# Bias seeded into the accumulation banks by ACT, in place of additions on GpSimd, in a two-layer graph kernel

## The chip, the cores and the metric

The kernel runs on one core of a Trainium2 chip. The metric is the device time of one execution in microseconds. Engines are named as in the profile: PE is TensorE's matmul, PEld its weight load, DVE is VectorE, ACT is ScalarE, POOL is GpSimd, SP is SyncE, which here only issues DMAs.

## The reference

There are 64 graphs of 256 nodes with 512 features, and one 256 x 256 adjacency matrix of zeros and ones. Two layers follow each other, each with a residual:

```python
h = jnp.maximum(_layernorm(x, axis=-1), 0.0)
# layer 0: masked scores, divided by the norm of their row
q, k, v = (jnp.einsum('bnd,ed->bne', h, W) for W in (Wq, Wk, Wv))
rel = adjacency.T[None, :, :] * jnp.einsum('bnd,bmd->bnm', q, k)
rel = rel / jnp.linalg.norm(rel, axis=2, keepdims=True)
x = x + jnp.einsum('bnm,bmd->bnd', rel, v)
h = jnp.maximum(_layernorm(x, axis=-1), 0.0)
# layer 1
y = jnp.einsum('nm,bmd->bnd', adj, h)
x = x + jnp.einsum('bnd,do->bno', y, weight) + bias
```

The last line holds what the change is about: the product of y with the weight, the bias of 512 values, and the addition to x.

## The kernel before

Work goes by pairs of graphs: 32 pairs, each of 512 rows in four chunks of 128 (TC = 4). Operands of products are split into three parts called u, l and s (upper, lower, and a third one for the cross terms), and `three` makes each product out of three passes over four chunks of the inner dimension, 12 matmuls of 512 columns, into one PSUM bank of 128 x 512.

`unit` is the frame of such a block. It takes the next of eight banks in rotation (`next_bank`), puts in the passes u and l, then an activation on ACT that multiplies the bank by ONE in place (L331), then the pass s, then a drain. The pass s of one block is recorded only after the passes u and l of the next block, so the scaling lies under other matmuls.

A pair goes through these stages:

- `h_rows`: statistics of the rows of the next pair on DVE (L259, L260, L263), then on ACT the square root (L265) and the normalised rows (L273).
- `g_stage`: four blocks of G, from h and a product of the query and key weights; each is split by ACT (gy_u, L232) and DVE (gy_s, L233, and gy_l, L235).
- `v_stage`: four blocks of V, two before and two after the scores, split in the same way into v_low and late_parts.
- `scores`: two blocks from G and h with 256 columns a matmul (h_u,gy_u, then h_l,gy_l, then hs,gy_s), multiplied on DVE by the adjacency (L406), their squares summed on ACT (L410) in the same bank.
- `turn_scores`: the scores turned by 16 DMAs on SP (L446) and DVE transposes (L452), and split (L462 to L464). In the first two pairs and the last one PE turns them.
- `attend`: four blocks of scores times V; DVE scales each by the row's norm and adds it to x in the tile `x_ring` (L487). There are two such tiles in turn.
- `layer_1`: statistics of the new x, then the normalised rows into `rel_s_raw` (L273), split by ACT (L507) and DVE (L508). After that POOL adds the bias, broadcast to 128 partitions in `bias_bc`, to each chunk of x (L511).
- `gather`, one pair late: four blocks that multiply by the adjacency, split by ACT (L241) and DVE (L242, L243) into the gy tiles again.
- `mix`, one pair late: four blocks of gy times the weight (w_u,gy_u; w_l,gy_l; w_s,gy_s); DVE adds each bank to x (L549). `store` writes x out by a DMA that POOL issues (L558).

The order of the instructions is not written by hand. Every step is recorded in a `Plan` with its engine, a cost in us, and keys that it reads and writes. `order` gives PE's steps due times by their own order and costs, works back to due times for all that they need, and then lists each engine's steps as they come ready, earliest due first. The engines run these lists in order, so a step that waits holds up all that stand behind it on its engine.

At the start the bias comes by a DMA on ACT's queue (L575) and is left alone until L511. Two versions of the pairs are compiled, for adjacencies that can and cannot be held exactly in the short format; this run takes the first, in which the tiles are called adjt_r and late_parts.

Of the kernel before, what the change touches and what calls it, by code (L numbers as in the profile page):

```python
# [12 lines left out]
AF = mybir.ActivationFunctionType  # L13
# [100 lines left out]
def kernel(  # L114
# [93 lines left out]
    V, A, G, SP = nc.vector, nc.scalar, nc.gpsimd, nc.sync  # L208
    count = {"bank": 0}

    def next_bank():
        n = count["bank"] % 8
        count["bank"] += 1
        return bank[n], ("bank", n)

    placed_all = [("blocks", j, k) for j in range(P // S) for k in range(P // S)]
# [102 lines left out]
        while waiting:  # L319
            waiting.pop(0)()  # L320

    def unit(plan, first, second, drain):

        ps, key = next_bank()
        for cost, fn, reads in first(ps):
            plan.add("PE", cost, fn, reads, [key])
        finish(plan)
        if second is None:
            drain(ps, key)
            return  # L330
        plan.add("ACT", 0.49, lambda: A.activation(ps, ps, AF.Copy, scale=ONE), [], [key])  # L331

        def rest():
            for cost, fn, reads in second(ps):
                plan.add("PE", cost, fn, reads, [key])
            drain(ps, key)
        waiting.append(rest)

    def three(left, right, names_l, names_r, cost, outs=None):


        def group(k, ds, begin):
            def first(ps):
                for d in ds:
                    for n, (o, lf, rt) in enumerate(outs(ps, k, d) if outs else [(ps, left(k, d), right(k, d))]):
                        mm(o, lf, rt, begin and d == ds[0] and n == 0)
            return first

        def first(ps):
            for k, ds, begin in ((0, (0, 1), True), (0, (2, 3), False), (1, (0, 1, 2, 3), False)):  # L350
                yield cost * len(ds), (lambda go=group(k, ds, begin): go(ps)), [
                    n for d in ds for n in (*names_l(k, d), *names_r(k, d))]

        def second(ps):
            ds = (0, 1, 2, 3)
            yield cost * len(ds), (lambda go=group(2, ds, False): go(ps)), [
                n for d in ds for n in (*names_l(2, d), *names_r(2, d))]
        return first, second
# [56 lines left out]
    def turn_scores(plan, i, by_pe=False):  # L415
        rn, name = norms[i % 2], f"rn{i % 2}"
        sums = [(name, b, k) for b in range(NB) for k in range(NC)]
        plan.add("ACT", 0.2, lambda: A.activation(rn, rn, AF.Sqrt), [], sums)
        plan.add("DVE", 0.12, lambda: V.reciprocal(rn, rn), [], sums)
        if by_pe:  # L420
            u, l = (part.rearrange("p b t k n -> p b (t k n)") for part in rel_p)
            for b in range(NB):
                ps, key = next_bank()

                def go(ps=ps, b=b):
                    for t in range(NC):
                        for k in range(NC):
                            nc.tensor.transpose(ps[:, ts(t * NC + k, P)], rel[:, b, k, ts(t, P)], ident)

                def third(b=b):  # L430
                    V.scalar_tensor_tensor(rel_third()[:, b].rearrange("p t k n -> p (t k n)"),
                                           f(l[:, b]), CROSS, f(u[:, b]), op0=ALU.mult, op1=ALU.subtract)
                plan.add("PE", 0.44, go, [("h_rel", b)], [key])
                plan.add("ACT", 0.49, lambda ps=ps, b=b: A.activation(
                    u[:, b], ps, AF.Copy, scale=NEAR), [key], [("rel_u", b)])
                plan.add("DVE", 0.63, lambda ps=ps, b=b: V.tensor_sub(
                    l[:, b], ps, f(u[:, b])), [key, ("rel_u", b)], [("rel_l", b)])
                plan.add("DVE", 0.6, third, [("rel_u", b), ("rel_l", b)],
                         [("raw", 0), ("raw", 1)] if not b else [("raw", 1)])
            return  # L440
        rv = rel.rearrange("p b k (t m) -> p (b k t) m", m=P)
        pv = placed.rearrange("p b k t n -> p (b k t) n")

        for j in range(P // S):
            for k in range(P // S):
                plan.add("SP", 0.65, lambda j=j, k=k: SP.dma_start(  # L446
                    out=pv[ts(j, S), :, ts(k, S)], in_=rv[ts(k, S), :, ts(j, S)]),
                    [("h_rel", 0), ("h_rel", 1)], [("placed", j, k)], lands=2.1)
        halves, rel_u, rel_l = ([(name, b) for b in range(NB)] for name in ("raw", "rel_u", "rel_l"))
        for b in range(NB):  # L450
            for k in range(NC):
                plan.add("DVE", 0.33, lambda b=b, k=k: V.transpose(  # L452
                    raw()[:, b].rearrange("p (t k n) -> p t k n", t=NC, k=NC)[:, :, k], placed[:, b, k]),
                    [("placed", j, t) for j in range(P // S) for t in range(P // S)] + [("h_rel", 2), ("h_rel", 3)], halves if not b and not k else halves[b : b + 1])

        def whole(ap):
            return ap.rearrange("p b t k n -> p (b t k n)")

        def flat_raw():
            return raw().rearrange("p b d -> p (b d)")  # L460
        u, l = (whole(part) for part in rel_p)
        plan.add("ACT", 0.96, lambda: A.activation(u, flat_raw(), AF.Copy, scale=NEAR), halves, rel_u)  # L462
        plan.add("DVE", 1.14, lambda: V.tensor_sub(l, flat_raw(), f(u)), [*halves, *rel_u], rel_l)
        plan.add("DVE", 1.14, lambda: V.scalar_tensor_tensor(  # L464
            whole(rel_third()), f(l), CROSS, f(u), op0=ALU.mult, op1=ALU.subtract), [*rel_u, *rel_l], halves)
# [28 lines left out]
    def layer_1(plan, i, exact):  # L494
        slot = i % 2
        relu, needs = norm(plan, i, 1, ring[slot], f"x{slot}")
        for c in range(TC):
            x_c = [(f"x{slot}", c), *needs]
            if not exact:
                plan.add("ACT", 0.72, lambda c=c: relu(changing("late", "h2", 8, D)[:, c], c), x_c,  # L500
                         keys("late", 12)[4:] if not c else [("late", 4 + c)])
                continue
            u, l = 3 + 2 * c, 4 + 2 * c
            k = [("raw", c % 2)]
            plan.add("ACT", 0.72, lambda c=c: relu(raw()[:, c % 2], c), x_c,
                     [("raw", 0), ("raw", 1)] if not c else k)
            plan.add("ACT", 0.53, lambda c=c, u=u: A.copy(late(u), raw()[:, c % 2]), k, [("late", u)])  # L507
            plan.add("DVE", 0.6, lambda c=c, u=u, l=l: V.tensor_sub(  # L508
                late(l), raw()[:, c % 2], f(late(u))), [*k, ("late", u)], [("late", l)])
        for c in range(TC):  # L510
            plan.add("POOL", 1.4, lambda c=c: G.tensor_tensor(  # L511
                ring[slot][:, c, :], ring[slot][:, c, :], bias_bc, ALU.add), [], [(f"x{slot}", c)])

    def gather(plan, i, exact):
        right = adjt[0]
# [24 lines left out]
    def mix(plan, i, blocks_of=range(4)):  # L540
        slot = i % 2
        for c in blocks_of:
            b = c // NC
            first, second = three(
                lambda k, d, c=c: gy[k][:, d, ts(c, P)], lambda k, d: w_p[k][:, d, :],
                gy_half(b), named("w_u", "w_l", "w_s"), MM)

            def drain(ps, key, c=c):
                plan.add("DVE", 0.6, lambda: V.tensor_add(  # L549
                    ring[slot][:, c, :], ps, ring[slot][:, c, :]), [key], [(f"x{slot}", c)])  # L550
                if i + 1 == NP:
                    plan.add("SP", 0.65, lambda: SP.dma_start(
                        out=outs[i][:, c, :], in_=ring[slot][:, c, :]), [(f"x{slot}", c)], [], lands=3.0)
            unit(plan, first, second, drain)

    def store(plan, i):
        slot = i % 2
# [60 lines left out]
    def first_turn(plan):  # L618

        u, l = h  # L620
        for d in range(DC):
            ps, key = next_bank()

            def go(ps=ps, d=d):
                for c in range(TC):
# [30 lines left out]

    def turn_wv(plan):
        for d in range(DC):
            ps, key = next_bank()

            def go(ps=ps, d=d):
                for e in range(DC):
                    nc.tensor.transpose(ps[:, ts(e, P)], wv_sb[:, e, ts(d, P)], ident)
            plan.add("PE", 0.44, go, placed_all, [key])
            split_right_ps(plan, ps, key, [lambda at, q=q: q[:, at, :] for q in wv_p],
                           [[("wv_u", d)], [("wv_l", d)], [("wv_s", d)]], d)
# [6 lines left out]
    def pairs(exact):  # L673
# [20 lines left out]
        h_turn(plan)  # L694
        h_parts(plan)
        split_w(plan)
        attend(plan, 0, exact)
        for i in range(1, NP):
            last = i + 1 == NP
# [63 lines left out]
```

## Time and profile before

| what | value |
|---|---|
| median of 3 runs | 1596.04 us (1594.61 to 1597.64) |
| the profiled execution | 1595.87 us |
| its span, first to last instruction | 1594.1 us |
| granted TensorE clock | 0.999 |
| instructions on PE, DVE, ACT, POOL | 8046, 2419, 1812, 167 |
| busy time of POOL, L511 alone | 216.2 us, 191.4 us |
| ACT's in-place scaling, L331 | 572 times, 581 ns each |
| reads and writes of HBM | 65 GB/s over the span |

Busy time of an engine is the union of its instructions. The end of a matmul is modelled, so PE can be called busy where the next matmul starts late; times lost on PE are read from the starts of matmuls in the timeline. A matmul of 512 columns appears as 128x512, its weights as 128x128. An entry like `x_ring<-bank,rn,x_ring` names what is written and what is read. Behind the bar stands the time that an engine sat idle before the group, and whom it waited for.

### The profile page before, as it was taken

The page shows a single profiled execution, that of the slowest core. Times are in us where ns is not written, and L with a number is a line of the kernel's source. Part 1 is how long each engine was busy: PE and PEld are TensorE (multiplying, and loading weights), DVE is VectorE, ACT ScalarE, POOL GpSimd, SP SyncE. Part 2 cuts the span into 40 slices and gives each one's busy share as a digit, 9 for nine tenths or more (in the row PEclk, how much of TensorE's full clock was granted, in tenths as well). Part 3 has the DMA queues.
Part 4 walks back from the last instruction along what each step waited for, and adds up shares of the span by engine and source line. Part 5 has one row for each costly group of instructions (what it writes and reads, how often), then busy time and mean ns, then how long its engine had stood idle before and what let it go on. Part 6 is the DMA issues. An engine that isn't in the chain of part 4 may idle for free.

```text
span 1594.1 us, 22542 instructions
## 1 busy us (share of the span) xinstructions
PE 1566.8 (98%) x8046; PEld 1327.2 (83%) x8046; DVE 1423.1 (89%) x2419; ACT 953.1 (60%) x1812; POOL 216.2 (14%) x167
## 2 busy tenths in 40 slices
PE   9999999999999999999999999999999999999998
PEld 6788888888888888888888888888888888888886
DVE  6998899988998988998989999889989889989886
ACT  5566566565566565665665565656665656656553
POOL 0011111011111011110111110111100111101111
PEclk9999999999999999999999999999999999999999
DMA  6421444324444334443234442344432344433311
GB/s 193 111 77 44 115 110 119 65 74 113 112 114 99 77 79 117 109 117 71 75 108 114 112 119 62 76 115 110 116 94 72 87 118 109 118 65 80 81 54 56
DMA packets 433130, 153.64 MB, mean 96 GB/s; under 512 B 389872, under 2 KB 390128, under 8 KB 433008
## 3 DMA queue, kind: packets, MB, share of 16 engines
q1 hardware_dynamic: 422784, 116.46, 30.9%
q0 software_dynamic: 8432, 32.51, 5.5%
q10 hardware_dynamic: 1792, 3.15, 0.5%
q8 instruction: 65, 1.06, 0.3%
q14 instruction: 57, 0.47, 0.1%
HBM read 70.78 MB, written 33.55 MB: 65 GB/s over the span
## 4 chain that ended last, share of the span: by engine, by line
DVE 43%; PE 42%; ACT 5%; SPq 4%; DMA 3%; issue 2%; DVEq 0%; ACTq 0%
PE bank L222 42%; DVE st L259 7%; DVE gy_l L235 7%; DVE x_ring L487 5%; DVE late_parts L508 5%; DVE gy_s L233 5%; DVE hs L302 4%; SPq L446 3%; DVE x_ring L549 2%; DVE mv L260 2%; ACT rel_s_raw L273 2%; SPq L287 1%; ACT gy_u L232 1%; DVE h_l L312 1%; DMA fresh<-in_x_dram 1%
## 5 line engine op out<-in xcount | busy, mean ns | idle before, releaser
L331 ACT ACTIVATE bank<-bank 128x512 f32<-128x512 f32 x572 | 332.3, 581 | 395.7 <-PE bank L222 393.3
L511 POOL TENSOR_TENSOR x_ring<-x_ring,bias_bc 128x512 f32<-128x512 f32 x128 | 191.4, 1515 | 382.3 <-ACT rel_s_raw L273 382.3
L558 POOL DMA_DIRECT2D out_dram<-x_ring x31 | 24.0, 774 | 978.5 <-DVE x_ring L549 978.5
L222 PE MATMUL bank<-wv_s,hs 128*128 128x512 f32 x512 | 138.5, 392 | 0.4 <-ACT bank L331 0.4
L222 PE MATMUL bank<-w_u,gy_u 128*128 128x512 f32 x512 | 138.0, 391 | 0.0
L222 PE MATMUL bank<-wv_u,h_u 128*128 128x512 f32 x512 | 137.7, 391 | 0.0
L222 PE MATMUL bank<-w_s,gy_s 128*128 128x512 f32 x512 | 137.4, 390 | 0.4 <-ACT bank L331 0.4
L222 PE MATMUL bank<-w_l,gy_l 128*128 128x512 f32 x512 | 137.4, 390 | 0.0
L222 PE MATMUL bank<-wv_l,h_l 128*128 128x512 f32 x512 | 137.3, 390 | 0.0
L222 PE MATMUL bank<-h_u,m_u 128*128 128x512 f32 x512 | 136.5, 389 | 0.3 <-DVE m_s L233 0.3
L222 PE MATMUL bank<-h_l,m_l 128*128 128x512 f32 x512 | 136.6, 389 | 0.1
L222 PE MATMUL bank<-hs,m_s 128*128 128x512 f32 x512 | 136.3, 389 | 0.0
L233 DVE SCALAR_TENSOR_TENSOR gy_s<-gy_u,bank 128x512 fp32r<-128x512 f32 x128 | 86.0, 674 | 41.9 <-ACT gy_u L232 41.8
L235 DVE SCALAR_TENSOR_TENSOR gy_l<-gy_s,gy_u 128x512 fp32r<-128x512 f32 x128 | 113.7, 890 | 4.3
L273 ACT ACTIVATE rel_s_raw<-x_ring,nb,rs 128x512 f32<-128x512 f32 x128 | 100.6, 810 | 24.9 <-DVE late_parts L508 15.6
L222 PE MATMUL bank<-adjt_r,late_parts 128*128 128x256 f32 x896 | 115.1, 280 | 0.0
L222 PEld LDWEIGHTS bank<-w_s,gy_s 128*128 128x128 f32 x512 | 95.9, 188 | 21.1 <-ACT bank L331 1.1
L222 PEld LDWEIGHTS bank<-w_u,gy_u 128*128 128x128 f32 x512 | 96.0, 188 | 20.8
L222 PEld LDWEIGHTS bank<-w_l,gy_l 128*128 128x128 f32 x512 | 96.1, 188 | 20.7
L222 PEld LDWEIGHTS bank<-wv_l,h_l 128*128 128x128 f32 x512 | 96.1, 188 | 20.5
L222 PEld LDWEIGHTS bank<-h_u,m_u 128*128 128x128 f32 x512 | 96.0, 188 | 20.5 <-ACT wv_u L232 0.5
L222 PEld LDWEIGHTS bank<-h_l,m_l 128*128 128x128 f32 x512 | 96.0, 188 | 20.4 <-DVE h_l L312 0.5
(109 smaller groups left out, 3226.9 us busy)
## 6 DMA issues: line engine op xcount, KB each, us to landing
fresh<-in_x_dram SPq DMA_DIRECT2D x31, 1024.0 KB, 5.9
blocks<-h_rel SPq DMA_DIRECT2D x496, 64.0 KB, 2.1
x_ring<-in_x_dram SPq DMA_DIRECT2D x31, 1024.0 KB, 7.9
out_dram<-x_ring POOLq DMA_DIRECT2D x31, 1024.0 KB, 5.4
h_rel<-h_rel SPq DMA_DIRECT2D x464, 32.0 KB, 1.9
blocks<-in_L_gnn_Wv_dram ACTq DMA_DIRECT2D x1, 1024.0 KB, 10.9
x_ring<-in_L_gnn_weight_dram SPq DMA_DIRECT2D x1, 1024.0 KB, 12.5
out_dram<-x_ring SPq DMA_DIRECT2D x4, 256.0 KB, 2.3
```

The lines of the kernel that those rows point to most:

```text
L222: nc.tensor.matmul(out, left, right, start=first, stop=True, skip_group_check=True)
L233: plan.add("DVE", 0.63, lambda: V.scalar_tensor_tensor(s(), f(u()), ONE, ps, op0=ALU.mult, op1=ALU.subtract), [*key, *ku], ks)
L235: plan.add("DVE", 0.6, lambda: V.scalar_tensor_tensor(l(), f(s()), -CROSS, f(u()), op0=ALU.mult, op1=ALU.add), [*ku, *ks], kl)
L259: V.bn_stats(st[:, c, :], src[:, c, :])
L260: V.bn_aggr(mv[:, c, :], st[:, c, :])
L273: A.activation(dst, src[:, c, :], AF.Relu, bias=nb[:, c : c + 1], scale=rs[:, c : c + 1])
L302: V.scalar_tensor_tensor(h_s[k], f(l), CROSS, f(u), op0=ALU.mult, op1=ALU.subtract)
L331: plan.add("ACT", 0.49, lambda: A.activation(ps, ps, AF.Copy, scale=ONE), [], [key])
L446: plan.add("SP", 0.65, lambda j=j, k=k: SP.dma_start(out=pv[ts(j, S), :, ts(k, S)], in_=rv[ts(k, S), :, ts(j, S)]), [("h_rel", 0), ("h_rel ...
L487: plan.add("DVE", 0.63, lambda: V.scalar_tensor_tensor(ring[slot][:, c, :], ps, rn[:, b, n : n + 1], ring[slot][:, c, :], op0=ALU.mult, op ...
L508: plan.add("DVE", 0.6, lambda c=c, u=u, l=l: V.tensor_sub(late(l), raw()[:, c % 2], f(late(u))), [*k, ("late", u)], [("late", l)])
L511: plan.add("POOL", 1.4, lambda c=c: G.tensor_tensor(ring[slot][:, c, :], ring[slot][:, c, :], bias_bc, ALU.add), [], [(f"x{slot}", c)])
```

## The change

The bias no longer goes through x. Once, at the start, ACT multiplies `bias_bc` by 1/ONE. Then each block of `mix` begins with a copy of `bias_bc` into its bank on ACT, and the block's first matmul adds to what lies there, where it overwrote it before. As the in-place scaling by ONE follows later for the whole bank, the bias comes out at its own size. The four POOL additions of each pair are gone. The function that hands out banks now remembers which of them were last filled by transposes, several to a bank, and passes over those for a block that begins with a bias.

```diff
-    def next_bank():
+    in_pieces = set()
+
+    def next_bank(turned=False, on=None):
+
+        while on is not None and count["bank"] % 8 in in_pieces:
+            count["bank"] += 1
         n = count["bank"] % 8
         count["bank"] += 1
+        (in_pieces.add if turned else in_pieces.discard)(n)
         return bank[n], ("bank", n)
...
-    def unit(plan, first, second, drain):
-
-        ps, key = next_bank()
+    def unit(plan, first, second, drain, on=None):
+
+
+        ps, key = next_bank(on=on)
+        if on is not None:
+            plan.add("ACT", 0.58, lambda: A.copy(ps, on), ["bias"], [key])
         for cost, fn, reads in first(ps):
...
-    def three(left, right, names_l, names_r, cost, outs=None):
+    def three(left, right, names_l, names_r, cost, outs=None, fresh_bank=True):
...
-            for k, ds, begin in ((0, (0, 1), True), (0, (2, 3), False), (1, (0, 1, 2, 3), False)):
+            for k, ds, begin in ((0, (0, 1), fresh_bank), (0, (2, 3), False), (1, (0, 1, 2, 3), False)):
...
-        for c in range(TC):
-            plan.add("POOL", 1.4, lambda c=c: G.tensor_tensor(
-                ring[slot][:, c, :], ring[slot][:, c, :], bias_bc, ALU.add), [], [(f"x{slot}", c)])
...
-                gy_half(b), named("w_u", "w_l", "w_s"), MM)
+                gy_half(b), named("w_u", "w_l", "w_s"), MM, fresh_bank=False)
...
-            unit(plan, first, second, drain)
+            unit(plan, first, second, drain, on=bias_bc)
...
         split_w(plan)
+        plan.add("ACT", 0.58, lambda: A.activation(bias_bc, bias_bc, AF.Copy, scale=1.0 / ONE), [], ["bias"])
         attend(plan, 0, exact)
```

In the three places where transposes fill a bank (`turn_scores` by PE, `first_turn`, `turn_wv`), `next_bank()` becomes `next_bank(turned=True)`.

More of the change, by code (lines that the diff above doesn't have):

```diff
@@ L422, in turn_scores @@
             for b in range(NB):
-                ps, key = next_bank()
+                ps, key = next_bank(turned=True)
                 def go(ps=ps, b=b):
@@ L621, in first_turn @@
         for d in range(DC):
-            ps, key = next_bank()
+            ps, key = next_bank(turned=True)
             def go(ps=ps, d=d):
@@ L658, in turn_wv @@
         for d in range(DC):
-            ps, key = next_bank()
+            ps, key = next_bank(turned=True)
             def go(ps=ps, d=d):
```

## The prediction

> **What bounds the kernel now.** I read the page first, then the groups by shape, the waits, and last the timeline of one pair in the middle of the run.
>
> ```profile
> PE 1566.8 (98%) x8046; PEld 1327.2 (83%) x8046; DVE 1423.1 (89%) x2419; ACT 953.1 (60%) x1812; POOL 216.2 (14%) x167
> ...
> DVE 43%; PE 42%; ACT 5%; SPq 4%; DMA 3%; issue 2%; DVEq 0%; ACTq 0%
> ```
>
> TensorE is busy 98%, and yet DVE holds 43% of the chain that ended last. Both can be: PE has hardly an idle slot, but where it has one, DVE is what it waits for. So the gain to be had is PE's lost time, not DVE's. The waits say where that is (columns: who waits for whom, us in total, times, longest):
>
> ```profile
> POOL x_ring L511 <- ACT rel_s_raw L273: 382.3, 63, 78.7
> ACT rs L265 <- DVE rs L263: 104.4, 62, 3.2
> ...
> PEld bank L222 <- DVE gy_l L235: 18.5, 30, 1.1
> ...
> PEld bank L222 <- ACT bank L331: 7.8, 23, 1.6
> ```
>
> The third line: thirty waits of the weight load (PEld) for gy_l, about one in each of the 31 pairs after the first. That is the second group of the scores, which needs the low part of the last block of G. The next question is why gy_l comes late. The groups by shape (count, then busy time and mean ns of one):
>
> ```profile
> L511 POOL TENSOR_TENSOR x_ring<-x_ring,bias_bc 128x512 f32<-128x512 f32 x128 | 191.4, 1515 | 382.3 <-ACT rel_s_raw L273 382.3
> ...
> L235 DVE SCALAR_TENSOR_TENSOR gy_l<-gy_s,gy_u 128x512 fp32r<-128x512 f32 x128 | 113.7, 890 | 4.3
> ...
> L508 DVE TENSOR_TENSOR late_parts<-rel_s_raw,v_low 128x512 fp32r<-128x512 f32 x32 | 54.0, 1686 | 1.1 <-ACT v_low L507 1.1
> ...
> L235 DVE SCALAR_TENSOR_TENSOR late_parts<-late_parts 128x512 fp32r<-128x512 f32 x64 | 44.2, 692 | 2.1
> ```
>
> The same L235 takes 692 ns on V's parts and 890 ns on gy's; L508 takes 1686 ns for one block in each pair. In the timeline they stand beside POOL's additions (start us, us):
>
> ```profile
> 804.01 2.98 POOL L511 TENSOR_TENSOR x_ring<-x_ring,bias_bc 128x512 f32<-128x512 f32 x2 [7.57 <-ACT rel_s_raw L273]
> ...
> 805.78 1.77 DVE L508 TENSOR_TENSOR late_parts<-rel_s_raw,v_low 128x512 fp32r<-128x512 f32 x1
> ...
> 808.48 3.00 POOL L511 TENSOR_TENSOR x_ring<-x_ring,bias_bc 128x512 f32<-128x512 f32 x2 [1.48 <-ACT rel_s_raw L273]
> 808.78 1.54 DVE L235 SCALAR_TENSOR_TENSOR gy_l<-gy_s,gy_u 128x512 fp32r<-128x512 f32 x1
> ...
> 811.74 0.87 PE L222 MATMUL bank<-h_l,gy_l 128*128 128x256 f32 x6
> ...
> 813.29 0.50 PE L222 MATMUL bank<-h_l,gy_l 128*128 128x256 f32 x2 [0.68 <-DVE gy_l L235]
> ```
>
> L508 ends 0.56 us after POOL's pair of additions, and L235 0.3 us after the first of the second pair: both look held until POOL lets go. PE then starts its seventh matmul 1.55 us after the first, where six take 0.68 (eight take 0.91 elsewhere in this pair): 0.87 us lost.
>
> **What the Trainium skill says.** SBUF — State Buffer, Terms: DVE and GpSimd share a port pair under an exclusive lock held for the whole instruction, and the loser blocks. GPSIMD Engine Reference, 8. Key points: it is DVE instructions with two SBUF inputs that contend. The trace agrees: L508 and gy_l's L235 read two tensors from SBUF and stretch to 1.77 and 1.54 us; L233, with one input in PSUM, keeps 0.69 us at 804.44 and the statistics L259, with one input, 0.68 us at 810.24, both beside POOL. One L235 at 805.16 keeps 0.69 us too; it starts about where the first addition ends and the second begins, so it may have slipped in between. ScalarE: Activation LUTs, What ACT_TABLE_LOAD costs: with immediate operands 186 ns + 0.833 ns an element, 613 ns for 512, and neighbours overlap by 93 ns. The trace has 605 ns for L507 and 1.12 us for two in a row, 0.52 apart. PSUM — Partial Sum Buffer, The four PSUM rules: writes by ACT leave the bits alone that decide whether a matmul adds or overwrites. That explains why the change skips banks last filled by transposes; no run here times it.
>
> **The change, part by part.** *Removed: 128 POOL additions.* POOL is off the path (it idles 382 us before them), but the two held DVE instructions go: 1.77 − 0.69 = 1.08 and 1.54 − 0.69 = 0.85, so 1.9 us a pair. Not all of it comes through, because DVE waits there for ACT's gy_u of the last block, which follows two L273 that wait for L508; following the queue by hand, the last gy_l moves from ending at 813.2 to about 811.6, so 1.6 us earlier. PE wanted it at 812.4. So the wait goes whole and 0.8 us is left over; in the pair at 521 us the wait is 0.49 and the margin larger. Worth: 18.5 us, and after each such wait the next two matmuls take 0.34 us for 0.23 (813.29 to 813.63), so 30 × 0.11 = 3.3. Together 21.8 us.
>
> *The second score block.* Its scaling (L331) stands on ACT behind L265, which waits up to 3.2 us for rs. With DVE 1.4 us earlier or more, L265 passes before PE has finished the group that L331 needs. The by-shape row of the weight loads for hs,gy_s gives 3.6 us of waits for L331; with the slow matmuls that follow them, some 15 × 0.11 = 1.6, that is 5.2 us.
>
> *Added: four ACT copies a pair, 128 in all.* Bounds for one: 0.52 (the step of back-to-back L507) and 0.605 (its mean alone); SBUF to PSUM at this size isn't in the trace, but 256 columns are (L410, 388 ns), and 256 × 0.833 ns more give 0.60. Below nothing is excluded, as each is an extra instruction. I take 0.52 in a queue: 2.1 us a pair, 67 us of ACT, which goes from 60% to about 65%. They hide only if their place allows. The new order on ACT puts all four between the squares of the scores (L410) and the square root of rn (L418): one behind each block's squares, one before the last gather block's gy_u, one behind the scaling of V block 2. Queued behind them are gy_u of the gather, that scaling and rn. By hand, on PE's clock without the waits: the first score's product starts at 817.7 instead of 818.44, as DVE is free; squares to 819.4; copy 819.9; gy_u, v_low, gy_u 821.4; squares 822.4; copy 822.9; gy_u, copy, gy_u 824.4; then V's scaling from 824.4 to 825.0. PE loads the weights that need it at 825.4. Margin 0.4 us. Before, it ran at 824.27 after 0.73 us of waiting: this waiting, and the earlier squares, are the cover. gy_u of the last gather blocks comes 0.8 to 1.2 us later; PE needs it only at 832. The fourth copy takes part of a 1.24 us wait. rn comes 2 us later but 0.9 us before DVE asks. So: 0.
>
> *Added wait:* each mix block's first matmul waits for its copy. The last is done at 825.4, the first block starts at 826.5, the fourth near 835. Behind that matmul stands all of PE, but the copies stand in ACT's queue before gy_u pieces that PE waits for anyway. The bank is free: it last held scores or gather blocks, drained there. 0.
>
> *Bookkeeping.* PE's and SP's orders are unchanged but for PE's last pair, so no DMA moves. There mix blocks go between gather blocks, where PE now waits 0.5 us at 1572.98 for L331: −0.5. On DVE one gather gy_s goes three places back and a V part moves up: 0. At the start ACT scales the bias, which lands at 10.95 + 9.7 = 20.65, where a weight split waited until 20.97: −0.2. No new table: L592 loads the only one, and copies run already.
>
> *What is late next.* The chain from the scores through SP's 16 moves (L446) to rel_l: L463 ends at 837.6, PE loads rel_l at 838.0. It starts and ends with PE, so it keeps its 0.4 us. Neighbouring pairs stand 48.4 us apart (the waits at 473.49 and 521.86). The round in which DVE is late takes 48.4 − 1.6 = 46.8 us without POOL, PE's own work 48.4 − 0.9 = 47.5, where 0.9 is the 27.0 us above over 30 pairs: PE becomes the bound, by 0.7 us.
>
> **Sum.** Against the profiled execution: 1595.87 (span 1594.1, 1.8 around it) − 21.8 − 5.2 − 0.5 − 0.2 = 1568.2. I give back 2 us for waits that stay in a few pairs: 1570; the median of the runs, 1596.04, is 0.2 higher, which changes nothing.
>
> **Rivals.** *ACT's queue eats half.* My margin at V's scaling is 0.4 us over ten hand-placed steps. If copies take 0.6 and other steps slip, PE waits about 0.45 us there in each pair: 1570 + 30 × 0.45 = 1583.5. For it: the tight margin; against: ACT still waits 1.2 us twice just behind. *Slower: the copies cost PE more than POOL did.* Same place, larger price. The old waits cost 0.9 us a pair, so this decides when V's scaling is over 0.4 + 0.9 = 1.3 us later than I count, that is copies of 0.85 us in the queue. At 1.0 us each: 4 × 0.48 − 0.4 − 0.9 = 0.6 us a pair, 1596 + 18 = 1614. Against it: L410 writes the same banks at the ordinary rate. *Nothing happens.* L508 and L235 are slow for reasons of their own, DVE stays as it is, copies hide: 1596. Against: the same lines take 0.69 us elsewhere in the same pair.
>
> **Chances.** Forecast 0.75, half-gain 0.13, nothing 0.05, slower 0.07. Range 1565 (no give-back, some small waits gone too) to 1586 (the half-gain case with its spread). Faster by over 0.2%, which is about what a measurement can tell: 0.88; within: 0.05; slower: 0.07.
>
> **What would show it.** Right: L235 on gy_l near 690 ns and L508 near 690 in all rows; the 30 waits for gy_l gone or under 2 us in total; pairs 47.5 us apart; PE busy over 98% of a shorter span; DVE some 60 us less busy. Wrong: PE waiting for L331 on wv_s,hs (half-gain or slower), for the bias copy at w_u,gy_u, or for rel_l; or L235 and L508 still long.

## The result, and the profile after

The changed kernel takes 1571.34 us, the median of 4 runs (1570.34 to 1572.01), where the kernel before takes 1595.97 (1594.61 to 1597.64) beside it: a ratio of 0.985, 95% interval 0.984 to 0.986. The forecast was 1570, in a range of 1565 to 1586. The profiled execution took 1571.74 us, with a span of 1570.0 and a granted clock of 1.0. The diff shifts the lines: the matmul helper is now L228 (L222 before), the splits L239 and L241 (L233, L235), the scaling by ONE L340 (L331), the statistics L265 (L259), the square root of rs L271 (L265), the split of layer 1 L516 and L517 (L507, L508). The new copy is L333.

The page first: busy time of each engine, and the shares of the chain that ended last.

```profile
PE 1557.2 (99%) x8046; PEld 1322.8 (84%) x8046; DVE 1357.6 (86%) x2419; ACT 1023.8 (65%) x1941; POOL 24.3 (2%) x39
...
PE 83%; SPq 5%; DVE 5%; DMA 4%; ACT 2%; issue 1%; ACTq 0%; DVEq 0%
PE bank L228 83%; SPq L293 4%; DMA fresh<-in_x_dram 2%; SPq L455 2%; ACT h_rel L279 1%; DVE st L265 1%; DMA bias_bc<-in_L_gnn_bias_dram 1%; DMA x_ring<-in_x_dram 1%; DMA h_rel<-h_rel 0%; DVE gy_s L239 0%; DVE gy_l L241 0%; ACT bank L340 0%; DVE h_rel L415 0%; DVE late_parts L239 0%; DVE mv L266 0%
```

DVE runs the same 2419 instructions in 65.5 us less (1423.1 before), and its share of the chain fell from 43% to 5%. PE holds 83%. SPq and DMA together hold 9%, hardly more than before (7%), but the shares by line show that it is another transfer: the block moves of h_rel (L293, L287 before) hold 4% for 1%, and the load of fresh 2% for 1%.

The waits of PE's weight loads (us in total, times, longest), from the list of waits:

```profile
PEld bank L228 <- ACT bank L340: 8.5, 22, 1.6
PEld bank L228 <- DVE late_parts L241: 1.8, 3, 1.2
PEld bank L228 <- DVE gy_l L241: 1.4, 4, 0.5
```

The 30 waits for gy_l, 18.5 us, are 4 waits and 1.4 us. The waits for the scaling look unchanged (7.8 before), but they have moved, which only the groups by shape show. First three of the kernel before, then those of the changed one:

```profile
L222 PEld LDWEIGHTS bank<-wv_s,hs 128*128 128x128 f32 x512 | 93.6, 188 | 19.7 <-ACT bank L331 1.2
L259 DVE BATCH_NORM_STATS2 st<-fresh 128x6 f32<-128x512 f32 x124 | 83.4, 672 | 1.6 <-DMA fresh<-in_x_dram 1.6
L222 PEld LDWEIGHTS bank<-hs,gy_s 128*128 128x128 f32 x512 | 64.0, 188 | 4.9 <-ACT bank L331 3.6
```

```profile
L228 PEld LDWEIGHTS bank<-wv_s,hs 128*128 128x128 f32 x512 | 92.8, 188 | 22.8 <-ACT bank L340 5.2
L265 DVE BATCH_NORM_STATS2 st<-fresh 128x6 f32<-128x512 f32 x124 | 83.7, 675 | 14.1 <-DMA fresh<-in_x_dram 13.8
L241 DVE SCALAR_TENSOR_TENSOR gy_l<-gy_s,gy_u 128x512 fp32r<-128x512 f32 x128 | 88.3, 692 | 4.3
L333 ACT COPY bank<-bias_bc 128x512 f32<-128x512 f32 x128 | 75.3, 589 | 3.7 <-DVE late_parts L239 1.0 <-DVE x_ring L555 0.6 <-DVE gy_s L249 0.2
L228 PEld LDWEIGHTS bank<-hs,gy_s 128*128 128x128 f32 x512 | 64.7, 189 | 0.7 <-ACT bank L340 0.2
L517 DVE TENSOR_TENSOR late_parts<-rel_s_raw,v_low 128x512 fp32r<-128x512 f32 x32 | 21.9, 684 | 1.2 <-ACT v_low L516 1.2
```

L241 on gy_l and the one slow L517 are back at 692 and 684 ns (890 and 1686 before). At hs,gy_s, the second score block, 3.6 us of waits for the scaling became 0.2. At wv_s,hs, V's third pass, 1.2 us became 5.2: that is the place the half-gain rival named. And DVE now waits 13.8 us for the load of the next x (fresh), where it waited 1.6.

Waits overlap with other things, so the sum is better made from PE alone: I took the time from each matmul's start to the next one's start and summed it by the tile of the first, so that a wait counts for the tile that stands in front of it. From PE's first to its last matmul, 23.8 us are gone:

| steps that begin at | us, after less before |
|---|---|
| h_l,gy_l (the wait for gy_l) | −18.1 |
| adjt_r,late_parts and hs,gy_s: the second score block and the tail's wait | −5.4 |
| the same tiles: steps inside the gather blocks (114 ns in the median for 118) | −2.2 |
| wv_l,h_l and wv_s,hs (V's scaling) | +2.3 |
| all others | −0.4 |

### The profile page after: what moved, and what is told of

Read it like the earlier page. It is cut to its first block, busy times and chain, and to the rows that moved or that the text cites. A ratio compares the mean times of both kernels' runs of the same rounds, so it can differ in the third digit from the quotient of the medians.

```text
span 1570.0 us, 22385 instructions
## 1 busy us (share of the span) xinstructions
PE 1557.2 (99%) x8046; PEld 1322.8 (84%) x8046; DVE 1357.6 (86%) x2419; ACT 1023.8 (65%) x1941; POOL 24.3 (2%) x39
## 4 chain that ended last, share of the span: by engine, by line
PE 83%; SPq 5%; DVE 5%; DMA 4%; ACT 2%; issue 1%; ACTq 0%; DVEq 0%
PE bank L228 83%; SPq L293 4%; DMA fresh<-in_x_dram 2%; SPq L455 2%; ACT h_rel L279 1%; DVE st L265 1%; DMA bias_bc<-in_L_gnn_bias_dram 1%; DMA x_ring<-in_x_dram 1%; DMA h_rel<-h_rel 0%; DVE gy_s L239 0%; DVE gy_l L241 0%; ACT bank L340 0%; DVE h_rel L415 0%; DVE late_parts L239 0%; DVE mv L266 0%
## 5 line engine op out<-in xcount | busy, mean ns | idle before, releaser
L340 ACT ACTIVATE bank<-bank 128x512 f32<-128x512 f32 x572 | 333.4, 583 | 321.5 <-PE bank L228 318.3
L228 PE MATMUL bank<-wv_s,hs 128*128 128x512 f32 x512 | 139.9, 395 | 0.2
L228 PE MATMUL bank<-w_u,gy_u 128*128 128x512 f32 x512 | 137.9, 391 | 0.0
L228 PE MATMUL bank<-wv_u,h_u 128*128 128x512 f32 x512 | 137.6, 390 | 0.0
L228 PE MATMUL bank<-w_s,gy_s 128*128 128x512 f32 x512 | 137.5, 391 | 0.0
L228 PE MATMUL bank<-w_l,gy_l 128*128 128x512 f32 x512 | 137.3, 390 | 0.0
L228 PE MATMUL bank<-wv_l,h_l 128*128 128x512 f32 x512 | 136.9, 389 | 0.0
L228 PE MATMUL bank<-h_u,m_u 128*128 128x512 f32 x512 | 136.5, 389 | 0.3 <-DVE m_s L239 0.3
L228 PE MATMUL bank<-h_l,m_l 128*128 128x512 f32 x512 | 136.6, 389 | 0.1
L228 PE MATMUL bank<-hs,m_s 128*128 128x512 f32 x512 | 136.3, 389 | 0.0
L239 DVE SCALAR_TENSOR_TENSOR gy_s<-gy_u,bank 128x512 fp32r<-128x512 f32 x128 | 86.2, 676 | 43.3 <-ACT gy_u L238 43.3
L228 PEld LDWEIGHTS bank<-w_u,gy_u 128*128 128x128 f32 x512 | 96.0, 188 | 20.8
L228 PEld LDWEIGHTS bank<-w_s,gy_s 128*128 128x128 f32 x512 | 95.7, 188 | 21.2 <-ACT bank L340 1.2
L228 PEld LDWEIGHTS bank<-w_l,gy_l 128*128 128x128 f32 x512 | 96.1, 188 | 20.7
L228 PEld LDWEIGHTS bank<-h_u,m_u 128*128 128x128 f32 x512 | 96.0, 188 | 20.5 <-ACT wv_u L238 0.5
L228 PEld LDWEIGHTS bank<-h_l,m_l 128*128 128x128 f32 x512 | 96.0, 188 | 20.4 <-DVE h_l L318 0.5
L228 PEld LDWEIGHTS bank<-wv_l,h_l 128*128 128x128 f32 x512 | 96.1, 188 | 20.2
L228 PEld LDWEIGHTS bank<-hs,m_s 128*128 128x128 f32 x512 | 96.1, 188 | 19.9
L228 PE MATMUL bank<-adjt_r,late_parts 128*128 128x256 f32 x896 | 112.8, 277 | 0.0
L228 PEld LDWEIGHTS bank<-wv_s,hs 128*128 128x128 f32 x512 | 92.8, 188 | 22.8 <-ACT bank L340 5.2
L228 PEld LDWEIGHTS bank<-wv_u,h_u 128*128 128x128 f32 x512 | 93.7, 188 | 17.8
L228 PEld LDWEIGHTS bank<-adjt_r,late_parts 128*128 128x128 f32 x896 | 107.5, 188 | 0.0
```

Source lines behind the costliest of these rows:

```text
L228: nc.tensor.matmul(out, left, right, start=first, stop=True, skip_group_check=True)
L239: plan.add("DVE", 0.63, lambda: V.scalar_tensor_tensor(s(), f(u()), ONE, ps, op0=ALU.mult, op1=ALU.subtract), [*key, *ku], ks)
```

## The experiments

The theory: two DVE instructions in each pair were held by GpSimd's additions, the copies hide, and nothing else changed. Its rivals: the two are slow for another reason, and something else in the change brought the gain; or the copies cost something, and the gain would be larger without them.

Each kernel is the changed one with the edit shown, unless it says otherwise. The ratio is to the kernel before, from runs on the same chip, with a 95% interval. "Lost on PE" is again taken from the starts of matmuls: what a step is longer than the median step of its kind; how the kinds are cut moves these sums by about half a us.

**1 and 2. GpSimd's additions back, with zeros.** If the additions were the cost, putting them back must bring the time back, with nothing else changed.

```diff
+        for c in range(TC):
+            plan.add("POOL", 1.4, lambda c=c: G.tensor_tensor(
+                ring[slot][:, c, :], ring[slot][:, c, :], wq_last, ALU.add), ["zero"], [(f"x{slot}", c)])
...
+        plan.add("POOL", 0.8, lambda: G.memset(wq_last, 0.0), [("m_u", k) for k in range(DC)], ["zero"])
```

The tile of zeros is wq_last, cleared once by GpSimd; the edit is that of run 2. In run 1 both lists of keys read were empty, and the tile was cleared before its last use, so a quarter of the query weights was zero in the product of the weights:

> The changed kernel with POOL's 128 additions put back where they stood, but of zeros, so that x doesn't change; the order on PE, DVE, ACT and SP is that of the changed kernel. Theory (POOL's additions hold two DVE instructions in each pair through the shared port, and that alone made gy_l late): 1596, up to 3 more for the waits at V's scaling, with L508's block and gy_l's L235 back near 1.7 and 1.5 us in each pair. Rival (the gain came from the new order of steps on DVE and ACT, or from the additions' place in the chain of writes to x): 1571 to 1575.

1601.34 us (1600.66 to 1602.93), ratio 1.004 (1.003 to 1.006), 2.3 us above what the theory allowed and far from the rival. As zeros might have changed more than intended, it was repeated with the tile cleared after its last use:

> As the first experiment, POOL adding zeros to x where it used to add the bias, with the tile of zeros filled only after the query weights that lay there have been used (in the first experiment it wiped out a quarter of them before use). Theory (the port): 1600 to 1602 again, since no time here depends on data. Rival (the wiped weights had a part in the time): under 1597.

1601.50 us (1600.10 to 1601.84), ratio 1.003 (1.002 to 1.005). PE, DVE, ACT and SP run the same instructions in the same order as in the changed kernel, so the 30.2 us between them are GpSimd's doing. By PE's steps they lie at h_l,gy_l (17.8), at adjt_r,late_parts and hs,gy_s (7.5) and at V's scaling (4.2). Groups by shape and the list of waits of the repeated run:

```profile
L241 DVE SCALAR_TENSOR_TENSOR gy_l<-gy_s,gy_u 128x512 fp32r<-128x512 f32 x128 | 114.0, 893 | 4.3
L228 PEld LDWEIGHTS bank<-wv_s,hs 128*128 128x128 f32 x512 | 91.4, 188 | 27.5 <-ACT bank L340 11.4
L517 DVE TENSOR_TENSOR late_parts<-rel_s_raw,v_low 128x512 fp32r<-128x512 f32 x32 | 54.0, 1686 | 1.2 <-ACT v_low L516 1.2
```

```profile
PEld bank L228 <- DVE gy_l L241: 18.2, 30, 1.1
```

893 and 1686 ns, 30 waits, 18.2 us: the kernel before has 890, 1686, 30 and 18.5. "Nothing happens" falls, since the two instructions are slow only beside GpSimd. The run is also 5.6 us slower than the kernel before. It has the additions and the copies, so with a late DVE the copies are not free: PE waits 11.4 us for V's scaling at wv_s,hs, where the kernel before waits 1.2.

**3. No copies, the bias left out.** The copies are taken away, and the first matmul of each mix block overwrites its bank again. Without copies the recorded plan comes out in another order on ACT and DVE: it is that of the kernel before, instruction by instruction, with ACT's one scaling of the bias added.

```diff
-                gy_half(b), named("w_u", "w_l", "w_s"), MM, fresh_bank=False)
+                gy_half(b), named("w_u", "w_l", "w_s"), MM)
...
-            unit(plan, first, second, drain, on=bias_bc)
+            unit(plan, first, second, drain)
```

> The changed kernel without the four ACT copies of a pair: the bias is left out altogether, and each mix block overwrites its bank as in the kernel before. Theory (the copies hide but for some 3 us of waits for V's scaling before wv_s,hs): 1568 to 1569. Rival (ACT's queue takes much of the gain): 1565 or less. Rival (copies cost nothing at all): 1571.

1570.07 us (1569.01 to 1571.13), ratio 0.984 (0.983 to 0.986): 1.3 us under the changed kernel, with ranges that overlap, and 1.1 above the upper end of the theory. PE's wait at wv_s,hs is 0.3 us, so those 5.2 us go with the copies:

```profile
L228 PEld LDWEIGHTS bank<-wv_s,hs 128*128 128x128 f32 x512 | 94.0, 188 | 19.0 <-ACT bank L340 0.3
```

Most of what they cost there is not gained when they go; other waits grow in this order (gy_l from 1.4 to 2.1, fresh from 13.8 to 16.7). How far that is due to the copies, and how far to the order, this run does not show.

The run says more when it is set beside the kernel before. On PE, DVE and SP the two run the same instructions in the same order, and on ACT too but for that one scaling; what is missing is GpSimd's 128 additions. So without any copy, and with no new order, taking the additions away is worth 1595.13 − 1570.07 = 25.1 us, which is all of the gain. With runs 1 and 2 the four cases are: additions alone 1596, neither 1570, copies alone 1571, both 1601. So the copies, with the order that comes with them, cost some 1 us where the additions are gone and 5.6 where they are not.

**4 and 5. Half of the additions back.** Chunks 0 and 1 (then 2 and 3) are added by GpSimd, and the other two come by copies. GpSimd here adds the bias divided by ONE, that is by 1 + 2^-12.

```diff
+        for c in (0, 1):
+            plan.add("POOL", 1.4, lambda c=c: G.tensor_tensor(
+                ring[slot][:, c, :], ring[slot][:, c, :], bias_bc, ALU.add), [], [(f"x{slot}", c)])
...
-            unit(plan, first, second, drain, on=bias_bc)
+            unit(plan, first, second, drain, on=None if c in (0, 1) else bias_bc)
```

> POOL adds the bias to chunks 0 and 1 of each pair as before, ACT seeds the banks of chunks 2 and 3 (POOL's two additions use the bias divided by ONE). So the first stretch of POOL stays, which holds L508 for 1.08 us. Theory (DVE had to become only 0.9 us faster in each pair for PE to be the bound, and L235 alone gives 0.85 at most): 1572 to 1577, with a remaining wait for gy_l of up to 0.2 us in a pair. Rival (each us of DVE counts alike): 1.08 of 1.93 come back, 1571 + 0.56 x 24.6 = 1585.

> POOL adds the bias to chunks 2 and 3 as before, ACT seeds the banks of chunks 0 and 1 (POOL's two additions use the bias divided by ONE). So the second stretch of POOL stays, which holds gy_l's L235 for 0.85 us. Theory (the margin decides, and L508's 1.08 us come through only in part, some 0.7): 1573 to 1579, with a wait for gy_l of 0.1 to 0.3 us in a pair. Rival (each us of DVE counts alike): 0.85 of 1.93 come back, 1571 + 0.44 x 24.6 = 1582.

Chunks 0 and 1: 1573.28 us (1571.88 to 1574.62), ratio 0.986 (0.984 to 0.988). Chunks 2 and 3: 1578.39 us (1576.97 to 1579.08), ratio 0.989 (0.988 to 0.991). The groups by shape of the first:

```profile
L241 DVE SCALAR_TENSOR_TENSOR gy_l<-gy_s,gy_u 128x512 fp32r<-128x512 f32 x128 | 89.3, 700 | 4.3
L228 PEld LDWEIGHTS bank<-h_l,gy_l 128*128 128x128 f32 x512 | 65.2, 189 | 1.7 <-DVE gy_l L241 1.4
L517 DVE TENSOR_TENSOR late_parts<-rel_s_raw,v_low 128x512 fp32r<-128x512 f32 x32 | 54.0, 1686 | 1.2 <-ACT v_low L516 1.2
```

and of the second:

```profile
L241 DVE SCALAR_TENSOR_TENSOR gy_l<-gy_s,gy_u 128x512 fp32r<-128x512 f32 x128 | 119.5, 936 | 4.3
L228 PEld LDWEIGHTS bank<-h_l,gy_l 128*128 128x128 f32 x512 | 65.1, 189 | 4.5 <-DVE gy_l L241 4.2
L517 DVE TENSOR_TENSOR late_parts<-rel_s_raw,v_low 128x512 fp32r<-128x512 f32 x32 | 21.9, 684 | 1.2 <-ACT v_low L516 1.2
```

Each two additions hold one of the two DVE instructions by about 1 us a pair and leave the other alone. The waits for gy_l are 1.4 us in the first kernel, as with no additions at all, and 4.2 in the second, where 18.5 stood with both holds. The kernels are 1.9 and 7.0 us slower than the changed one, 8.9 together, where all four additions cost 25.1 (without copies) to 30.2 (with all). These two kernels have two copies a pair and their own order on ACT and DVE, so the single figures are good to a us or two; in the first, PE is already 3.3 us late at 186 us and loses nothing more from there to the end. But the gap to 25 is far larger: the cost is not a sum. With both holds gy_l came some 0.8 us late in the prediction's pair (813.2 for 812.4), and taking either of them away brings it about back to its time. That this margin is the reason is argued from the one pair.

**6. Each copy twice.**

```diff
-            plan.add("ACT", 0.58, lambda: A.copy(ps, on), ["bias"], [key])
+            plan.add("ACT", 0.58, lambda: (A.copy(ps, on), A.copy(ps, on)), ["bias"], [key])
```

> The changed kernel with each ACT copy of the bias made twice, one behind the other, at the same place in the same order. Theory (the copies fill ACT's slack between the squares of the scores and V's scaling to the brim, and what comes on top is paid by PE): three further copies stand ahead of that scaling, 3 x 0.52 = 1.5 us in each of 29 pairs, less 0.1 of slack: 1571 + 40 = 1605 to 1620, all of it in waits of wv_s,hs for the scaling. Rival (copies are hidden with room to spare): 1571 to 1576.

1623.49 us (1621.46 to 1629.32), ratio 1.018 (1.016 to 1.021), 3 us beyond the upper end. Groups by shape:

```profile
L333 ACT COPY bank<-bias_bc 128x512 f32<-128x512 f32 x256 | 150.6, 589 | 7.5 <-DVE late_parts L239 1.0 <-DVE x_ring L555 0.4 <-DVE gy_s L249 0.2
L228 PEld LDWEIGHTS bank<-wv_s,hs 128*128 128x128 f32 x512 | 92.3, 190 | 71.3 <-ACT bank L340 55.0
```

Three copies stand ahead of V's scaling in a pair, so doubling them adds three of 0.5 us in the queue, 1.5 us (the sum of the prediction's slower rival counts four). PE lost 50.7 us there (at wv_l,h_l and wv_s,hs), where it lost 3.0 with single copies: 47.7 more, 1.5 us in each of 31 pairs. So the three second copies were paid in full. ACT is only 68% busy and has no slack at this place: the slower rival had the right place, and here, with twice the work in it, it comes true. (Some 4 of the 52 us lie elsewhere; the granted clock was 0.994 to 0.998 in these runs.)

**7. GpSimd with one input.** GpSimd adds the constant 0 to each chunk, and so reads one tensor and not two.

```diff
+            plan.add("POOL", 1.4, lambda c=c: G.tensor_single_scalar(
+                ring[slot][:, c, :], ring[slot][:, c, :], 0.0, op=ALU.add), [], [(f"x{slot}", c)])
```

> The changed kernel with 128 POOL instructions at the place of the old additions that add the constant 0 to x, so with one tensor input in place of two. Theory A (any POOL instruction holds DVE's two-input instructions for as long as it runs): L508's block and gy_l's L235 are held until it ends; if it takes 0.7 us in place of 1.5, they are held half as long, DVE loses some 0.5 to 0.9 us a pair, and the time is 1573 to 1582. Theory B (only POOL's second input collides): both stay at 0.69 us, and the time is 1571 to 1573.

1574.09 us (1572.34 to 1574.90), ratio 0.986 (0.985 to 0.988). Groups by shape, and then the timeline of the pair in the middle (start us, us):

```profile
L520 POOL TENSOR_SCALAR x_ring<-x_ring 128x512 f32<-128x512 f32 x128 | 196.4, 1548 | 358.5 <-ACT rel_s_raw L279 358.5
L517 DVE TENSOR_TENSOR late_parts<-rel_s_raw,v_low 128x512 fp32r<-128x512 f32 x32 | 33.9, 1061 | 1.1 <-ACT v_low L516 1.1
```

```profile
793.12 3.18 POOL L520 TENSOR_SCALAR x_ring<-x_ring 128x512 f32<-128x512 f32 x2 [7.82 <-ACT rel_s_raw L279]
...
794.88 1.10 DVE L517 TENSOR_TENSOR late_parts<-rel_s_raw,v_low 128x512 fp32r<-128x512 f32 x1
...
797.03 2.95 POOL L520 TENSOR_SCALAR x_ring<-x_ring 128x512 f32<-128x512 f32 x2 [0.72 <-ACT rel_s_raw L279]
797.21 0.97 DVE L241 SCALAR_TENSOR_TENSOR gy_l<-gy_s,gy_u 128x512 fp32r<-128x512 f32 x1
```

Neither expectation holds: the time lies in the range of theory A, but its mechanism does not. GpSimd's instruction is no shorter than the one with two inputs (1548 and 1517 ns in the mean), but DVE is held 0.28 to 0.42 us and not until it ends: L517 is done at 795.98, 0.32 us before GpSimd. Such holds cost 2.7 us, or 2.1 by the ratios, where those with two inputs cost 30.2. The run also answers a rival that runs 1 and 2 left standing, the additions' place in the chain of writes to x: here GpSimd writes x at the same place and for as long, with the same orders on PE, DVE, ACT and SP, and the time hardly changes.

**8 to 10. What is late next.** Two waits are new in the changed kernel: V's scaling, and fresh. Run 8 moves the third and fourth copy behind the scaling of V's second half (by a key that the copy now reads). Run 9 changes only SP's queue: the load of fresh is issued ahead of the 16 moves of h_rel and not behind them. Run 10 has both.

```diff
-            plan.add("ACT", 0.58, lambda: A.copy(ps, on), ["bias"], [key])
+            plan.add("ACT", 0.58, lambda: A.copy(ps, on), ["bias", *behind], [key])
...
-            unit(plan, first, second, drain, on=bias_bc)
+            unit(plan, first, second, drain, on=bias_bc, behind=[("late", 6)] if c >= 2 else [])
```

```diff
+            if getattr(fn, "kind", "") == "fresh":
+                place = [m for m, g in enumerate(out) if getattr(g, "kind", "") == "place"][-16:]
...
+                    out.insert(place[0], fn)
...
```

> Two of the four bias copies of a pair stand behind the first scaling of V's second half in ACT's queue; TensorE's order and SyncE's are those of the changed kernel. If the copies ahead of V's scaling are what TensorE waits for at wv_s,hs (5.2 us of waits for L340 at that tile, some 3 us of lengthened steps in all), these go and the time is 1568 to 1569.5, with the wait at wv_s,hs under 1.5 us. Rival: the copies themselves are not late, V's scaling is bound by TensorE's filling of its banks; then no difference, 1571.

> Only the order of SyncE's queue is changed: in a pair's steady part the load of x (fresh) is issued ahead of the 16 block moves and not behind them. VectorE's 13.8 us of idle time before L265 should fall below 3. If VectorE's wait for that load is what makes gy_l and the scaling chain late next (1.4 us at gy_l, and part of the rest), the time is 1568.5 to 1570. Rival: VectorE has room again since the additions are gone, so its wait costs nothing and the time stays at 1571; or the block moves come late by one load and h_l waits, then 1573 or more.

> Both edits together: the two copies behind V's scaling and the load ahead of the block moves. If both waits are separate the gains add: 1566 to 1568. If only the copies matter, as for the copies alone, 1568 to 1569.5. Rival: neither matters, 1571.

| run | us | ratio to before | step from pair to pair, us | lost on PE at V's scaling | at h_l,gy_l |
|---|---|---|---|---|---|
| changed kernel | 1571.34 (1570.34 to 1572.01) | 0.985 (0.984 to 0.986) | 47.80 | 3.0 | 1.8 |
| 8, late copies | 1574.65 (1573.34 to 1576.56) | 0.987 (0.986 to 0.989) | 47.67 | 0.1 | 1.6 |
| 9, early load | 1566.03 (1565.53 to 1566.80) | 0.982 (0.981 to 0.983) | 47.57 | 0.2 | 0.0 |
| 10, both | 1572.16 (1571.78 to 1572.69) | 0.986 (0.984 to 0.987) | 47.57 | 0.1 | 0.0 |

(The step is the mean from pair 2 to pair 29.) The early load gains 5.3 us, or 4.9 by the ratios, more than was expected, and it alone clears both places. PE, DVE and ACT keep the order of the changed kernel in run 9. The chain of the changed kernel that leads there, from its timeline (start us, us):

```profile
792.67 0.62 SPq L257 DMA_DIRECT2D fresh<-in_x_dram  x1
...
798.54 0.69 DVE L265 BATCH_NORM_STATS2 st<-fresh 128x6 f32<-128x512 f32 x1 [0.72 <-DMA fresh<-in_x_dram]
...
801.60 0.50 PE L228 MATMUL bank<-h_l,gy_l 128*128 128x256 f32 x2 [0.34 <-DVE gy_l L241]
...
805.93 0.20 ACT L271 ACTIVATE rs<-rs 128x4 f32<-128x4 f32 x1 [3.21 <-DVE rs L269]
806.04 0.58 ACT L340 ACTIVATE bank<-bank 128x512 f32<-128x512 f32 x1
...
814.29 1.20 PE L228 MATMUL bank<-wv_s,hs 128*128 128x512 f32 x4
```

SP is busy with the 16 moves until 792.6, issues the load at 792.67, and DVE waits for it until 798.54. The same wait makes the last gy_l late at PE (801.60), rs late at ACT, and with it all that stands behind L271 on ACT: the scaling of the second score block, the squares, the copies, V's scaling. In run 9, which is 5 us ahead at this place, the load is issued at 774.87, before the moves. Its groups by shape, and its shares of the chain:

```profile
L237 PEld LDWEIGHTS bank<-wv_s,hs 128*128 128x128 f32 x512 | 93.7, 188 | 19.1 <-ACT bank L354 0.5
L276 DVE BATCH_NORM_STATS2 st<-fresh 128x6 f32<-128x512 f32 x124 | 83.6, 674 | 0.6 <-DMA fresh<-in_x_dram 0.6
```

```profile
PE 93%; DVE 4%; DMA 1%; ACT 1%; SPq 0%; issue 0%; ACTq 0%; DVEq 0%
```

So V's scaling is late only where two things meet: copies ahead of it, and a DVE that came late. Taking away either clears it. The late copies do so as well (0.1), and shorten the step from pair to pair by 0.13 us: PE is 3.1 us ahead of the changed kernel when the last pair begins. But there it loses 5.5 us, and the run is 3.3 us slower. In the last pair the copies stand behind layer 1's rows and splits on ACT, and PE waits for them once (start us, us):

```profile
1542.44 1.62 ACT L333 COPY bank<-bias_bc 128x512 f32<-128x512 f32 x3
...
1543.59 0.77 PEld L228 LDWEIGHTS bank<-w_u,gy_u 128*128 128x128 f32 x4 [4.07 <-ACT bank L333]
```

The expectation missed that, as it looked only at the steady pairs. Run 10 is level with run 9 up to its last pair, within 0.3 us in the steady part, and then loses 6.4 us in the same way (1566 to 1568 was expected). So beside the early load the late copies bring nothing, and their price is in the last pair alone.

**11. The early load without copies** (bias left out, as in run 3).

> The load of x ahead of the block moves, and no bias copies; the bias is left out of the sum. It is to be set beside 1566.0, the same order of loads with the copies. If the copies are free once VectorE does not wait for the load, the time is 1565.5 to 1566.5. Rival: the copies cost the 1.3 us that leaving them out gained with the late load, then 1564 to 1565.

1565.20 us (1565.07 to 1565.94), ratio 0.981 (0.980 to 0.983). That lies between what was expected of free copies and of the rival. Set against 1566.03, the copies cost 0.8 us; since the two were not run side by side, their ranges overlap, and the order on ACT and DVE differs as in run 3, it may be nothing. This run does not settle it. From PE's first matmul to its last the two profiled executions differ by 0.3 us. The step from pair to pair is 47.55 us, against 47.57 with copies.

**12. The kernel before with the early load.**

> The kernel before with only SyncE's queue changed: the load of x ahead of the block moves. If the load came to bind only when the additions on GpSimd were gone (VectorE waits 1.6 us for it in the kernel before, 14.1 us in the changed one), no difference: 1595 to 1596.5. Rival: the early load is worth its 5.3 us there too, 1590 to 1592.

1595.27 us (1593.89 to 1597.20), ratio 1.000 (0.999 to 1.001). So the load became a bound only when the additions went. With DVE held by GpSimd, its wait for the load is 1.6 us in the kernel before and 2.8 in run 2, for 13.8 in the changed kernel.

## Why the prediction was right, and where it was off

*The wait for gy_l.* That the additions hold the two DVE instructions, and that PE waits for gy_l because of it, is shown by runs 2 to 5. The size: 21.8 us were forecast, PE's steps there gave 18.1, and 1.8 stays. That makes 19.9, so the 3.3 us for the matmuls after the waits were 1.9 too much.

*The second score block and the tail.* Forecast 5.2 + 0.5, measured 7.5. The steps at which PE waited give 5.4 of it (3.3 in front of hs,gy_s, 1.7 inside it, 0.5 in the tail), close to the forecast. The other 2.2 the prediction did not have: the matmuls of the gather blocks follow each other at 118 ns in the median in the kernel before and at 114 in the changed one. Run 2 has 117, run 5 has 118 and run 4 has 114, so the longer step comes with the two additions that hold gy_l's L241 and not with the other two; its cause stays open.

*The copies at 0.* The hand-made margin of 0.4 us at V's scaling was the weakest step, and all of it was used up. From the first score's product to V's scaling I counted 6.7 us; the trace has 6.89 (806.75 to 813.64). From its start to PE's load I had 1.0 us, and PE's matmul starts 0.65 after it. The first is 0.2 us and the second 0.35 us against the margin. So the scaling ends at 814.24 and the matmul stands at 814.29, with 0.08 us lost. PE lost 3.0 us in all at this place, about a fifth of the half-gain rival's 13.5, and taking the copies out gains 1.3. That rival named the right place and queue; its size was off, as PE loses more than 0.05 us there in only 11 of the pairs, and run 6 shows how little was missing.

*One copy.* 0.52 us in a queue was taken; the steps in ACT's queue are 0.51 to 0.53, and the mean alone is 589 ns. The Trainium skill, ScalarE: Activation LUTs, What ACT_TABLE_LOAD costs, gives an estimate of 613 for 512 elements, 4% more than the trace. ACT's share is 65%, as said.

*What is late next.* This step named the chain through SP's moves of the scores to rel_l, and that one did keep its place (waits for rel_l stay under 2 us in all). What came instead was SP's other block of moves, with the load of fresh behind it: a resource that I had counted as unmoved, since SP's order did not change. SP's order stayed, but DVE came to the load earlier and found it not there. My 46.8 us for a round of DVE assumed all its inputs in time. That cost some 5 us (run 9) and is the reason why the step is 47.8 and not close to 47.5.

*The sum.* Before the give-back it was 1568.2, and the profiled execution took 1571.74, 3.5 more: 3.7 at gy_l, 2.3 at V's scaling, less 1.8 at the second score block and the tail, less 0.6 for the rest. The give-back of 2 us, a bare margin, covered a little over half of that. So the mechanism is right, and the total is right partly by luck: terms that miss in opposite directions cancel.

*The lock.* The prediction cited the Trainium skill, SBUF — State Buffer, Terms: held for the whole instruction. With two inputs on GpSimd the trace agrees. In all 67 holds of the kernel before, DVE's instruction ends 0.55 us after GpSimd's, so with 0.69 us of its own it starts work 0.14 us before GpSimd's recorded end. (The prediction read 0.56 us for L508 and 0.3 for L235. The second is a misreading: it took half of the 3.00 us of two additions, and the first of them ends at 809.77, 0.55 us before L235.) With one input it does not agree: DVE's instruction ends 0.33 us before GpSimd's, and the measurement decides. The L235 that "may have slipped in between" did so, at GpSimd's cost: the addition that starts beside it takes 1.73 us, the one before it 1.29.

## What to carry to other kernels

Ask of an engine that does little and is off the path whether its instructions lengthen another engine's: the same line with two durations (692 and 890 ns) is the sign. The proof is to take that work away or put it back with zeros while the order on all other engines stays. A hold is paid only beyond the margin (25 to 30 us for all four additions, 2 and 7 for each half), so estimate them together. And when an engine gets faster, go through the arrival of each of its inputs, those whose order does not change first: here some 5 us lay in one load behind 16 small moves, and moving it, which did nothing for the old kernel, gave 1566.0 us, the fastest version with the whole computation.

## What the runs showed of the hardware that was not expected

The hold goes both ways. In the kernel before, GpSimd's addition of two 128x512 tensors takes 1.28 to 1.31 us in the 64 cases in which no DVE instruction with two SBUF inputs works at its start. In the 64 others one does, and it takes 1.73 to 1.77 us (1.53 once). The mean of 1515 ns is the mean of these two groups.

With one tensor input GpSimd is not faster. Run 7 has the same two groups, 1.48 to 1.49 us (95 cases) and 1.67 to 1.75 (33), so undisturbed it takes 0.2 us longer than with two. Yet it holds a DVE instruction with two SBUF inputs for 0.3 to 0.4 us only: L517 took 1061 ns beside it in the mean, 1686 beside the addition of two tensors, and 684 alone. In all 64 holds of run 7 DVE's instruction ends 0.33 to 0.34 us before GpSimd's, so it gets through about 1.02 us before that end, at a fixed distance from the end and not from the start: 0.47 us after the start of an instruction of 1.49 us (797.03 to 797.49 for L241), 0.70 us after the start of one of 1.72 us (L517). Whether the hold ends with the reading of the one input is argued from this, not shown.
